# When the previous image's feed-forward runs inside the next image's convolution-attention, and where the weights are loaded

## Chip, core and metric

The kernel runs on one core of one Trainium2 chip. The metric is the time of one execution in microseconds of device time; the number to be predicted is the median of the runs. TensorE is called PE in the profile, VectorE DVE, ScalarE ACT, GpSimd POOL and SyncE SP. Matrix products read from SBUF and write to PSUM; every engine works through its own queue, and engines wait for one another through semaphores.

## The reference

Two layers on an input of 4 images with 128 channels and 64 x 64 = 4096 positions, all in float32. Cut to what matters:

```
# layer 0, per image: group norm (32 groups of 4 channels), 1x1 convolutions, attention over positions
g = groupnorm(x)                           # one mean and variance per 4 channels
e1, e2 = prelu(w1 @ g + b1), prelu(w2 @ g + b2)     # 64 x 4096
asm = prelu(wa @ g + ba)                            # 128 x 4096
x = x + softmax(e1.T @ e2, axis=2) @ asm.T

# layer 1, on tokens t = (position, channel)
z = layernorm(t) in 16 heads of 8; q = qz_ring(z + rx)      # cosines and running products
ctx = softmax(q @ q.T / sqrt(8)) @ q      # keys and values are q too
x1 = ln(layernorm(t) + ctx @ w_comb.T + b_comb) * g1 + be1
f  = relu((cos(x1[:8]) * cos(ry)) @ f1.T + fb1) @ f2.T + fb2
t2 = t + ln(x1 + f) * g2 + be2
# last: batch-normed linear map of layernorm(t2), then a sigmoid recurrence over tokens
out = t2 + scan(sigmoid(Wx_t + y @ V.T))
```

The attention runs over all 4096 tokens of an image, in 16 heads of 8 channels.

## The kernel before, in words

The four images go through three stages one after the other: first_stage (group norm, convolutions, the first attention, and from its results the tokens q), second_stage (the attention of 16 heads, the longest part) and third_stage (feed-forward). Only the last image has a third_stage of its own. The feed-forward of image n is otherwise run inside first_stage of image n + 1.

The order of the instructions on TensorE, ScalarE and VectorE within first_stage and second_stage is the order in which the program writes them (a manual schedule); TensorE executes in that order, so an instruction whose operand is late holds up what is behind it. In the rest of the program (the loads at the start, third_stage, the POOL and SP queues in first_stage) a planner chooses the order by its own estimates, with the program's order as priority.

Work is written as generators that yield between steps, so that pieces of several jobs can be laid between one another:

- layer0 (L324) is the main job of first_stage. It calls meanwhile after each of its groups: 4 calls in the e1 convolutions, 4 in e2, 4 in the asmT convolution (calls 1 to 12), then 16 calls for each of the 8 blocks of 512 positions (calls 13 to 140). In a block it writes two score products (L387, exponential on ScalarE L395, sum on VectorE L400 or L403), then one weighing (L410) of an earlier pair before each of the two calls; the first two calls come before there is anything to weigh.
- tokens (L468) makes the tokens of one block of 512 positions out of layer0's result, in 17 steps: transposes px, pt, layer norm, the cosines, products q (L542), transposes pq. One of them is begun every 16 calls, from call 30 on; each call takes one step of the oldest (two in the last block).
- feed_forward (L975) treats 512 tokens of the image before, in 27 steps (counted from 0): transposes pc and copy cT (0), product pw and sum v with x1 (1, L998), statistics (2), norm (4), z and cosines (6, 8), copy zs (9), transposes pz (11), products ph with relu to hT (13, 14), product pf (16), u and statistics (17), norm (19), t2 and statistics (21, L1071), norm of w (23, L1075), transposes pt2 with copy t2T and store to DRAM (24), transposes pl with the copy last or every (25), product pwx and its statistics (26). Its PSUM tiles come from a pool of two buffers.
- in_steps (L1169) keeps up to two feed-forwards active in first_stage and begins a new one every 14 steps; third_stage keeps up to eight and begins one every step. There the norms are done by ScalarE.
- mirrored (L769) ends the attention of a block: many small copies on POOL and a sum into own (L792). The last three blocks of an image leave three result functions (L797, L798: own divided by its denominators, into q), which first_stage calls at the calls named in L1206.

At the start, load (L135) and load_row issue all weights on POOL's queue: first w1, w2, b1, b2, wa, a1, a2, aa and ba; then the weights of later parts, rx to beta, 23 of them; then identity and constants; and last the group matrix grp, which two affine selects on POOL (L198) cut out of a constant. norm_stats (L303) needs it: image 0's two products pg and pv, on which its group norm hangs. PSUM pairs (ps_pair, two buffers) carry convolutions and scores alternately.

Of the kernel before, what the change touches and what calls it, by code (L numbers as in the profile page):

```python
# [10 lines left out]
F32 = mybir.dt.float32  # L11
F32R = mybir.dt.float32r
AF = mybir.ActivationFunctionType
ALU = mybir.AluOpType
# [12 lines left out]
def kernel(  # L27
# [32 lines left out]
    P = 128  # L60
# [71 lines left out]
    BIG, MID, HALF, ONE = (P, S), (P, 2, IC), (P, IC), (P, IC)  # L132


    def load(ap, name, shape=None):  # L135
        t = const.tile(list(shape or ap.shape), F32, tag=name, name=name)
        nc.gpsimd.dma_start(out=t, in_=ap)
        return t

    def load_row(ap, name):  # L140
        return load(ap.partition_broadcast(P), name, (P, ap.shape[-1]))
# [23 lines left out]
    for i, b in enumerate((b1_sb, b2_sb)):  # L165
        t = const.tile([P, 1], F32, tag=f"minus_b{i}", name=f"minus_b{i}")
        nc.vector.tensor_scalar(t, b, -1.0, None, ALU.mult)
        minus_b.append(t)
    rx_bc = load_row(rx, "rx_bc")
    wc_sb, bc_bc = load(w_combT, "wc_sb"), load_row(b_comb, "bc_bc")  # L170

# [2 lines left out]
    nc.gpsimd.memset(f1_sb, 0.0)  # L174
    nc.gpsimd.memset(ry_sb, 0.0)
    for f in range(NF):
        nc.gpsimd.dma_start(out=f1_sb[ds(32 * f, D), :], in_=f1T[:, ts(f, P)])
        nc.gpsimd.dma_start(out=ry_sb[ds(32 * f, D), :], in_=ry)
    fb1_sb, f2_sb, fb2_bc = load(fb1, "fb1_sb"), load(f2T, "f2_sb"), load_row(fb2, "fb2_bc")
    g1_bc, be1_bc = load_row(g1, "g1_bc"), load_row(be1, "be1_bc")  # L180
    g2_bc, be2_bc = load_row(g2, "g2_bc"), load_row(be2, "be2_bc")
# [10 lines left out]
    nc.vector.memset(half_pi, math.pi / 2)  # L192
    minus_half = const.tile([P, NT], F32, tag="minus_half", name="minus_half")
    nc.vector.memset(minus_half, -0.5)

    grp = const.tile([P, P // 4, 4], F32, tag="grp", name="grp")
    nc.vector.memset(grp, 0.25)
    for sign, base in ((1, 0), (-1, 3)):  # L198
        nc.gpsimd.affine_select(
            out=grp,  # L200
            in_=grp,
            compare_op=ALU.is_ge,
            fill=0.0,
            base=base,
            pattern=[[-4 * sign, P // 4], [0, 4]],
            channel_multiplier=sign,
        )
    grp = grp.rearrange("p a b -> p (a b)")

    V = D + 1  # L210
    t2_dram = dram.tile([N * P, S], F32, tag="t2", name="t2_dram")
# [763 lines left out]
    def feed_forward(im, i, t2_rows, last, final):  # L975


        n, cols = im["n"], ts(i, IC)

        def norm(dst, src, mv, rstd, name):  # L980
            if final:
                normalise_act(blocks(dst), blocks(src), mv, rstd, TG, f"{name}{n}_{i}")
            else:
                normalise(blocks(dst), blocks(src), mv, rstd, TG)

        x1 = get("x1", f"fx1_{n}_{i}")
        nc.sync.dma_start(out=x1, in_=im["x1"][:, cols])
        nc.gpsimd.tensor_tensor(blocks(x1), blocks(x1), row4(bc_bc), ALU.add)
        pt = transposed(blocks(im["q"][:, cols]), f"pc{n}_{i}")
        cT = get("fhalf", f"cT{n}_{i}")  # L990
        nc.scalar.copy(cT, pt)
        yield

        pa = one_psum(f"pw{n}_{i}")
        for k in range(TG):
            nc.tensor.matmul(pa[:, ts(k, P)], cT[:, ts(k, P)], wc_sb, start=True, stop=True)
        v = get("fhalf", f"v{n}_{i}")
        nc.vector.tensor_tensor(v, pa, x1, ALU.add)  # L998
        yield
        mv, rstd = token_stats(blocks(v), TG, 1e-5, f"v{n}_{i}")  # L1000
        yield
        yield
        norm(v, v, mv, rstd, "v")
        nc.gpsimd.tensor_tensor(blocks(v), blocks(v), row4(g1_bc), ALU.mult)
        nc.gpsimd.tensor_tensor(blocks(x1), blocks(v), row4(fb2_bc), ALU.add)
        yield
        yield

        z, zk, zr = (
            small.tile([P, TG, D], F32, tag=name, name=f"{name}{n}_{i}") for name in ("z", "zk", "zr")  # L1010
        )
        be1_z = be1_bc[:, 0:D].unsqueeze(1).broadcast_to([P, TG, D])
        nc.vector.tensor_tensor(z, blocks(v)[:, :, 0:D], be1_z, ALU.add)
        steps = cos_steps(zr, z, zk, zr)
        for _ in range(3):
            next(steps)
        yield
        yield
        next(steps, None)
        yield  # L1020
        zs = get("fhalf", f"zs{n}_{i}")
        nc.vector.tensor_copy(
            zs.rearrange("p (k r d) -> p k r d", k=TG, d=D),
            zr.unsqueeze(2).broadcast_to([P, TG, P // D, D]),
        )
        yield
        yield
        pz = transposed(blocks(zs), f"pz{n}_{i}")
        zT = get("fhalf", f"zT{n}_{i}")
        nc.scalar.copy(zT, pz)  # L1030
        yield
        yield
        hs = []
        for f0 in range(0, NF, 2):
            phs = [one_psum(f"ph{n}_{i}_{f}") for f in range(f0, f0 + 2)]
            hs.append(get("hT", f"hT{n}_{i}_{f0}"))
            for j in range(2):
                rows = ds(32 * (f0 + j), D)
                nc.tensor.matmul(phs[j], f1_sb[rows, :], zT[rows, :], start=True, stop=True)
            for j in range(2):  # L1040
                bias = fb1_sb[:, f0 + j : f0 + j + 1]
                nc.scalar.activation(hs[-1][:, j, :], phs[j], AF.Relu, bias=bias)
            yield
        yield
        x0 = get("fhalf", f"fx0_{n}_{i}")
        nc.sync.dma_start(out=x0, in_=im["x0"][:, cols])
        po = one_psum(f"pf{n}_{i}")
        for k in range(TG):
            for f in range(NF):
                nc.tensor.matmul(  # L1050
                    po[:, ts(k, P)],
                    hs[f // 2][:, f % 2, ts(k, P)],
                    f2_sb[:, f, :],
                    start=f == 0,
                    stop=f == NF - 1,
                )
        yield

        u = im["q"][:, cols]
        nc.vector.tensor_tensor(u, po, x1, ALU.add)  # L1060
        mv, rstd = token_stats(blocks(u), TG, 1e-5, f"u{n}_{i}")
        yield
        yield
        norm(u, u, mv, rstd, "u")
        nc.gpsimd.tensor_tensor(blocks(u), blocks(u), row4(g2_bc), ALU.mult)
        nc.gpsimd.tensor_tensor(blocks(u), blocks(u), row4(be2_bc), ALU.add)
        yield
        yield

        t2 = get("fhalf", f"t2_{n}_{i}")  # L1070
        nc.vector.tensor_tensor(t2, u, x0, ALU.add)  # L1071
        mv, rstd = token_stats(blocks(t2), TG, 1e-5, f"w{n}_{i}")
        yield
        yield
        norm(u, t2, mv, rstd, "w")  # L1075
        yield
        pt = transposed(blocks(t2), f"pt2_{n}_{i}")
        t2T = get("fhalf", f"t2T{n}_{i}")
        nc.scalar.copy(t2T, pt)
        nc.sync.dma_start(out=t2_rows[:, cols], in_=t2T)  # L1080
        yield
        pt = transposed(blocks(u), f"pl{n}_{i}")
        tokens_i = last(n, i, pt)
        yield
        if n != "r":
            token_products(n, i, tokens_i)
# [99 lines left out]
    def first_stage(im, before):  # L1186


        n = im["n"]


        ffn = dict(x1=(HALF, 2), fhalf=(HALF, 6), hT=(MID, 2))
        sums = dict(sums=(MID, 2), half=(HALF, 2), thalf=(HALF, 6))
        rest = dict(e=(BIG, 2), big=(BIG, 1), mid=(MID, 5))
        pools = {**ffn, "gap": ((P, GAP), 1), **rest, **sums}
        psum = dict(ps_acc=(ONE, 1), ps_pair=(MID, 2), ps_one=(ONE, 2), ps_tok=(ONE, 1))
        engines = {nc.tensor.engine, nc.scalar.engine, nc.vector.engine}
        with stage(f"conv{n}", **pools, **psum), tc.manual_schedule(engines=engines):
            nc.gpsimd.memset(get("gap", f"gap{n}")[:, 0:1], 0.0)
            own, calls = [], [0]  # L1200
            step_late = in_steps(feed_forwards(before) if before else [], 14, 2)

            def meanwhile(steps=1):

                calls[0] += 1
                if before and calls[0] in (13, 15, 17):  # L1206
                    before["left"].pop(0)()
                for _ in range(steps):
                    step_first(own)
                if calls[0] > 8:  # L1210
                    step_late()

            norm = im["norm"] or list(norm_stats(n, im["xs"]))[-1]
            layer0(
                n,
                im["xs"],
                im["q"],
                norm,
                n == "r",
                lambda ic, sums: own.append(tokens(im, ic, sums)),  # L1220
                meanwhile,
            )
            *own, tail = own
            for g in own:
                for _ in g:
                    pass
            while step_late():
                pass
            while not next(tail):
                pass  # L1230
        return tail
# [308 lines left out]
```

## Time and profile before

| what | us |
|---|---|
| median of 3 runs (7298.4 to 7300.03) | 7299.96 |
| the profiled execution itself | 7298.87 |
| its span in the profile | 7297.2 |
| image 0: scores, windows 59 to 435 us | 376 long, TensorE busy 370.5, mean clock 1.00 |
| image 1: scores with feed-forward, 1715 to 2222 us | 507 long, TensorE busy 462.9, mean clock 0.96 |
| image 2: the same, 3504 to 4010 us | 506 long, TensorE busy 469.2, mean clock 0.97 |
| image 3: the same, 5285 to 5785 us | 500 long, TensorE busy 456.0, mean clock 0.96 |
| pwx of the last feed-forward starts | 7185.48 |

Busy time is the time in which an engine executed; the clock is the share of TensorE's full rate that was granted. The windows' bounds are the first score product and about the first product of the attention that follows. In a timeline each row gives start, duration, engine, line, operation and count, and in brackets how long the engine had been idle before and what ended the wait. In a table of waits each row gives the waiting group, the group it waited for, the total in us, how many times, and the longest.

### The profile page before, as it was taken

What the parts mean: (1) busy time and instruction counts of PE and PEld (TensorE: products, weight loads), DVE (VectorE), ACT (ScalarE), POOL (GpSimd) and SP (SyncE); (2) the same over time, 40 slices, a digit from 0 to 9 for tenths busy, and PEclk for the clock granted to TensorE, in tenths of its full rate; (3) what the DMA queues carried; (4) which work ended last, traced back from release to release, by engine and by line L of the source; (5) the groups of instructions that cost most, each with busy time, mean ns of one, the idle gap of its engine ahead of it and who ended that gap; (6) DMA issues with size and microseconds to landing.
All of it is one profiled execution on the core that took longest, in us unless ns stands there. A gap on an engine that the chain in (4) does not pass through costs nothing. (4 is left out here: it accounts for less than half of the span.)

```text
span 7297.2 us, 224976 instructions
## 1 busy us (share of the span) xinstructions
PE 7005.9 (96%) x93198; PEld 3505.6 (48%) x93198; DVE 5997.3 (82%) x8097; ACT 5906.1 (81%) x11647; POOL 2795.8 (38%) x9860
## 2 busy tenths in 40 slices
PE   8999999999999999999989999999999999999977
PEld 3345555554444555554444455555444455555546
DVE  5678899886778899889677998889877788889974
ACT  3479999995448999999444999999844599999976
POOL 1024445333323444443423354444522343444542
PEclk9999999999999999999999999999999999999988
DMA  1010000000111000000011100000001110000012
GB/s 28 32 35 24 28 22 21 21 9 25 35 34 47 30 20 21 21 23 20 21 34 44 38 21 20 21 27 19 18 22 39 39 37 21 21 26 27 11 59 105
DMA packets 81598, 212.81 MB, mean 29 GB/s; under 512 B 8801, under 2 KB 8833, under 8 KB 79793
## 3 DMA queue, kind: packets, MB, share of 16 engines
q1 hardware_dynamic: 77312, 186.68, 7.5%
q8 instruction: 733, 12.01, 0.7%
q10 hardware_dynamic: 2016, 10.49, 0.4%
q14 instruction: 305, 2.49, 0.1%
q0 software_dynamic: 1232, 1.14, 0.1%
HBM read 141.65 MB, written 56.62 MB: 27 GB/s over the span
## 5 line engine op out<-in xcount | busy, mean ns | idle before, releaser
L882 ACT ACTIVATE e<-s 128x1024 f32<-128x1024 f32 (+1 forms) x3480 | 2946.7, 889 | 63.9 <-PE s L870 39.8
L689 DVE STREAM_TRANSPOSE t<-e 128x1024 f32<-128x1024 f32 x2240 | 2586.5, 1207 | 6.6 <-ACT e L882 4.3
L702 PEld LDWEIGHTS misc<-t,mirror 128*32 128x32 f32 x57344 | 1662.9, 110 | 1410.7 <-issue 1347.7
L702 PE MATMUL misc<-t,mirror 128*32 128x128 f32 x57344 | 1995.7, 273 | 28.5 <-DVE later L716 21.3
L882 ACT ACTIVATE xs<-s 128x1024 f32<-128x1024 f32 (+1 forms) x2152 | 1835.2, 893 | 32.8 <-PE s L870 19.6
L689 DVE STREAM_TRANSPOSE t<-xs 128x1024 f32<-128x1024 f32 x1344 | 1558.2, 1207 | 2.2 <-ACT xs L882 0.8
L723 PE MATMUL acc<-e,q_aug 128*32 128x512 f32 x11360 | 1518.4, 606 | 0.0
L870 PE MATMUL s<-queries,keys 32*128 32x512 f32 x9216 | 1218.3, 495 | 4.1 <-ACT e L882 2.7
L765 POOL COPY own<-o 32x36 f32<-32x36 f32 x2048 | 434.3, 212 | 1724.4 <-DVE o L757 1644.1
L395 ACT ACTIVATE p<-s 128x1024 f32<-128x1024 f32 x512 | 497.8, 1022 | 626.6 <-PE s L387 625.4
L410 PE MATMUL acc<-p,asmT 128*128 128x512 f32 x2048 | 981.3, 612 | 0.0
L723 PE MATMUL acc<-xs,q_aug 128*32 128x512 f32 x7072 | 942.2, 605 | 0.0
L403 DVE TENSOR_TENSOR total<-total,p 128x1024 f32<-128x1024 f32 x448 | 580.8, 1296 | 325.6 <-ACT p L395 301.8
L870 PEld LDWEIGHTS s<-queries,keys 32*128 32x128 f32 x9216 | 480.7, 182 | 491.3 <-issue 366.1
L790 POOL COPY other<-turned 32x64 f32<-32x64 f32 x1904 | 449.1, 236 | 631.3 <-DVE turned L780 552.8
L659 POOL COPY mirror<-q 32x128 f32<-32x128 f32 x2048 | 598.8, 292 | 239.1 <-PE misc L702 151.2
L882 ACT ACTIVATION_READ_ACCUMULATOR e<-s 128x1 f32 x2880 | 650.5, 226 | 0.0
L410 PEld LDWEIGHTS acc<-p,asmT 128*128 128x128 f32 x2048 | 364.6, 192 | 520.7 <-issue 516.1
L387 PE MATMUL s<-e,e 64*128 64x512 f32 x2048 | 526.6, 633 | 24.8 <-DVE asmT L301 21.2
L716 DVE TENSOR_TENSOR later<-later,misc 128x128 f32<-128x128 f32 (+1 forms) x576 | 162.4, 282 | 369.9 <-PE misc L702 365.9
L750 POOL COPY by_token<-by_key 32x4 f32<-32x4 f32 x2016 | 373.9, 185 | 85.0
L723 PEld LDWEIGHTS acc<-e,q_aug 128*32 128x32 f32 x11360 | 225.7, 108 | 347.8 <-issue 330.1
(258 smaller groups left out, 4764.0 us busy)
## 6 DMA issues: line engine op xcount, KB each, us to landing
keys<-parts_dram SPq DMA_DIRECT2D x256, 256.0 KB
queries<-parts_dram SPq DMA_DIRECT2D x1024, 32.0 KB
fx<-x_dram SPq DMA_DIRECT2D x64, 256.0 KB
x_dram<-x SPq DMA_DIRECT2D x56, 256.0 KB
xs<-in_x_dram SPq DMA_DIRECT2D x16, 512.0 KB
t_dram<-t2T SPq DMA_DIRECT2D x32, 256.0 KB
t2s<-t_dram SPq DMA_DIRECT2D x16, 512.0 KB
parts_dram<-high SPq DMA_DIRECT2D x28, 256.0 KB
```

The source lines that it names most:

```text
L387: nc.tensor.matmul(s[:, j, :], e2[rows, ts(2 * jp + j, P)], e1[rows, ts(ic, IC)], start=True, stop=True,)
L395: nc.scalar.activation(p, s, AF.Exp)
L403: nc.vector.tensor_tensor(state[ic], state[ic], p, ALU.add)
L410: nc.tensor.matmul(state["acc", ic], asmT[:, ts(2 * jp + j, P)], p[:, j, :], start=jp == 0 and j == 0, stop=jp == NP - 1 and j == 1,)
L659: nc.gpsimd.tensor_copy(wv[ts(a, 32), s, :, :, ts(a, D)], own[ts(s, 32)])
L689: nc.vector.transpose(group["e"][h][:, k, :], es[h])
L702: nc.tensor.matmul(state["acc"][ts(2 * x + h, 32), :], state["w"][:, QT * (s // 4) + TG * x + s % 4, h, :], state["e"][h][:, :, ds(IC * x ...
L723: nc.tensor.matmul(it["in"]["acc"][ts(2 * h + x, 32), :], it["qa"][:, ds((2 * it["tiles"][x] + h) * V, 32)], it["e"][h][:, ts(x, IC)], sta ...
L765: nc.gpsimd.tensor_copy(own[ts(s, 32), ts(x, 4), h, :], ov[ts(2 * h + x, 32), s, :, 0:V])
L790: copy(to[ts(k, 32), h], tv[ts(2 * x + h, 32), k])
L870: nc.tensor.matmul(ss[h][:, x, :], keys[unit[x] // QT].bitcast(F32R)[r, ts(unit[x] % QT, P)], queries[b].bitcast(F32R)[r, :], start=True, ...
L882: nc.scalar.activation(es[h][:, ts(x, IC)] if split else es[h], ss[h][:, x, :] if split else ss[h].rearrange("p x c -> p (x c)"), AF.Exp, ...
```

## The change

It has three parts. In the load code, grp is built right after the first weights, and the loads from rx to beta are issued by ScalarE instead of POOL (the two memsets that precede the loads of f1 and ry stay on POOL). In feed_forward, pt2 with its copy and store is put ahead of the norm of w, in the same step as that norm; the number of steps stays 27. In meanwhile, the feed-forward of the image before takes no step in calls 1 to 12 (before: 1 to 8), then one step in each call and two in every eighth; the second and third left result are called at calls 16 and 19 (before: 15 and 17).

```diff
+    loader = [nc.gpsimd]
     def load(ap, name, shape=None):
         t = const.tile(list(shape or ap.shape), F32, tag=name, name=name)
-        nc.gpsimd.dma_start(out=t, in_=ap)
+        loader[0].dma_start(out=t, in_=ap)
         return t
...
-    rx_bc = load_row(rx, "rx_bc")
...
-    nc.vector.memset(minus_half, -0.5)
     grp = const.tile([P, P // 4, 4], F32, tag="grp", name="grp")
...
     grp = grp.rearrange("p a b -> p (a b)")
+    loader[0] = nc.scalar
+    rx_bc = load_row(rx, "rx_bc")
+    wc_sb, bc_bc = load(w_combT, "wc_sb"), load_row(b_comb, "bc_bc")
...
+    nc.gpsimd.memset(f1_sb, 0.0)
+    nc.gpsimd.memset(ry_sb, 0.0)
+    for f in range(NF):
+        nc.scalar.dma_start(out=f1_sb[ds(32 * f, D), :], in_=f1T[:, ts(f, P)])
+        nc.scalar.dma_start(out=ry_sb[ds(32 * f, D), :], in_=ry)
...
+    nc.vector.memset(minus_half, -0.5)
@@ feed_forward
         yield
         yield
-        norm(u, t2, mv, rstd, "w")
-        yield
         pt = transposed(blocks(t2), f"pt2_{n}_{i}")
         t2T = get("fhalf", f"t2T{n}_{i}")
         nc.scalar.copy(t2T, pt)
         nc.sync.dma_start(out=t2_rows[:, cols], in_=t2T)
+        norm(u, t2, mv, rstd, "w")
+        yield
         yield
         pt = transposed(blocks(u), f"pl{n}_{i}")
@@ first_stage
                 calls[0] += 1
-                if before and calls[0] in (13, 15, 17):
+                if before and calls[0] in (13, 16, 19):
                     before["left"].pop(0)()
                 for _ in range(steps):
                     step_first(own)
-                if calls[0] > 8:
+                for _ in range(0 if calls[0] <= 12 else 2 if calls[0] % 8 == 0 else 1):
                     step_late()
```

## The prediction

> **What bounds the kernel now.** I read the page's busy table and slices first, then the timeline of the start, then the timelines and waits of TensorE in the stretches where feed-forward is mixed into the next image's first stage.
>
> ```profile
> PE 7005.9 (96%) x93198; PEld 3505.6 (48%) x93198; DVE 5997.3 (82%) x8097; ACT 5906.1 (81%) x11647; POOL 2795.8 (38%) x9860
> ...
> PE   8999999999999999999989999999999999999977
> ```
>
> TensorE is busy almost everywhere, so time is to be had only where it idles or runs slowly. The change touches four such places: the start, the three stretches of slices 10-12, 20-22 and 29-31, and the last feed-forward. In the long attention stretches the windows show TensorE busy for 181.9 us of 182 and nothing is changed.
>
> The start, from its timeline (columns: start us, duration us, engine, line, operation, count, idle before and its releaser):
>
> ```profile
> 9.15 0.54 POOL L137 DMA_DIRECT2D aa_sb<-in_aa_dram  x1 [0.27 <-DMA w_sb<-in_w2T_dram]
> ...
> 14.38 0.37 DVE L310 BATCH_NORM_AGGREGATE gmv<-gst 128x2 f32<-128x48 f32 x1
> ...
> 23.96 0.53 POOL L199 TENSOR_SCALAR_AFFINE_SELECT grp<-grp 128x128 f32<-128x128 f32 x1
> ...
> 24.54 0.58 PE L312 MATMUL pg<-gmv,grp 128*128 128x1 f32 x2 [24.54 <-POOL state L1433]
> ```
>
> The reader is to see that the statistics are there at 14.75 us, but the first matmul waits until 24.5 for the group matrix, which POOL makes only after issuing all loads at 0.50 to 0.58 us each. Everything after hangs on this matmul.
>
> The beginning of the scores of images 1 and 3, timelines of TensorE and VectorE:
>
> ```profile
> 1704.30 0.60 PE L273 MATMUL pc<-ident,q 128*128 128x128 f32 x4
> ...
> 1720.97 0.69 DVE L998 TENSOR_TENSOR v<-pw,fx 128x512 f32<-128x512 f32 x1 [10.45 <-POOL own L792]
> ...
> 1727.15 3.78 PE L387 MATMUL s<-e,e 64*128 64x512 f32 x8 [8.94 <-DVE asmT L301]
> ...
> 1735.70 1.99 PE L387 MATMUL s<-e,e 64*128 64x512 f32 x8
> ...
> 5297.61 3.78 PE L387 MATMUL s<-e,e 64*128 64x512 f32 x8 [9.18 <-DVE asmT L301]
> ```
>
> The second feed-forward step writes v (L998) while POOL still finishes the attention before it (its last mirrored sum, L792, ends at 1720.94). VectorE waits 10.45 us there with the last two asmT groups queued behind it; TensorE then waits 8.94 us for a PSUM buffer that asmT has to release. In image 2 the same place waits only 1.27 us.
>
> Inside the score loop, TensorE's waits of image 1 from 1727 us on:
>
> ```profile
> PE pl L273 <- DVE q L255: 11.8, 3, 4.4
> PE pq L273 <- DVE q L542: 9.2, 2, 6.2
> ...
> PE pc L273 <- ACT hT L1042: 5.4, 7, 0.8
> ...
> PE ph L1039 <- DVE wx_stats L1092: 2.1, 1, 2.1
> PE pt L273 <- DVE t L1071: 1.5, 2, 0.8
> ```
>
> These are moments when VectorE is two or more calls behind TensorE. The windows give TensorE 462.9 us busy of 507 in image 1's scores, at a mean clock of 0.96.
>
> **What the Trainium skill says.** (1) "TensorE: Matmul & The Clock Gate", Part 1: the array falls to half rate after an idle window of about 3.4 us and needs as long to recover. The trace agrees: after the wait of 8.94 us eight L387 matmuls took 3.78 us, otherwise 1.99. A wait above 3 us thus costs 2 to 3 us more. (2) The table that opens that page: ScalarE, VectorE and GpSimd have strictly first-in-first-out queues. That is the 10.45 us case. (3) "Trainium Kernel Development and Optimization", Key Constraints: DMAs from SP, ACT and POOL use the same 16 DMA engines, so another issuer saves issue time only. No run here shows a change of issuer for the same load; the trace shows 0.54 us for a POOL issue and a median of 0.47 us for ScalarE's loads of every.
>
> **The change part by part.**
>
> *Start.* 23 loads leave POOL's queue and the two selects of grp (0.55 + 0.53 us) come right after ba_row, whose issue ends at 10.69. So grp is there at about 11.8, before gmv at 14.75, and pg starts near 14.9: 24.5 - 14.9 = 9.6 us less. Now gmv is late next: its last two bn_stats stand in VectorE's queue behind the wait for aa_sb (landed 13.0). ScalarE issues 23 loads at about 0.47 us = 11 us; its first real work, L294, was at 31.7 and would be at 22. The loads of f1 wait for POOL's memset (now near 12 us), with the rest queued behind them: ScalarE is done near 12 + 20 x 0.47 = 21.4, just in time. The loads now overlap those of x: the windows show the DMA engines full (1.03) from 4 to 8 us. If aa_sb, or the fb_bc add and ry steps in VectorE's queue, land later, up to 6 us are lost. I take -8.5 (ends: -10 and -3).
>
> *First scores.* Calls 9 to 12 lose their steps: the transposes pc (0.60) and products pw (1.06) leave the asmT phase and come between the first score pairs. Worked out for image 1: asmT matmuls end at 1714.84 - 1.66 = 1713.2; two score pairs of 1.1 us with a wait of 1.1 for the exponential between them, 1716.5; pc 0.6; wait for cT on ScalarE (exponential 1.0 + copy 0.6) to 1718.3; pw 1.06; two pairs 2.0 and two weighings 3.7: the next L387 at 1725.1 against 1735.7. -10.6, half-clock included. VectorE still waits until 1720.94 for v, but reaches it only at 1719.4, with asmT done. The two left results (reciprocal and product, 0.25 + 0.29 us each) at calls 16 and 19 find POOL done. Image 3 the same, image 2 has only about -1 to gain. Sum -21 (ends -24 and -12).
>
> *Rate.* From call 13 on, one step a call and two in each eighth: after call c, c - 12 + floor(c/8) - 1 steps are done. Eight feed-forwards of 27 steps, 14 apart, need 7 x 14 + 27 = 125: before, the last was in call 133, now in call 123 of 140. The instructions are the same. What a doubled call does: two successive steps lie in one call, so a consumer follows its producer without a score pair between. The doubled steps are 9m - 15 and 9m - 14. By their place in the feed-forward those that hurt TensorE are 39/40 (pwx waits for the copy of pl, 1.09 us less 0.6 of pz: 0.5), 66/67 (pl one call closer to its norm; a call is about 4 us: 0 to 4, I take 2.5), 84/85 (pw waits for cT: 0.6) and 111/112 (the second ph waits for two relus of 0.6: 1.3). Sum 5 us per image.
>
> VectorE's lag: tokens use it in bursts, a new one every 16 calls from call 30 on. Of 27 feed-forward steps, 1 to 9 with 15 to 23 beside them carry nearly all of the 13.5 us of VectorE work. Before, pl falls 14, 12 and 10 calls after a token start in the three cases that wait, and 16, 8, 2 or fewer in those that don't. Now it falls at 5, 2, 14, 10, 7, 3, 16 and 12: again three in 10 to 14 and one at 16 (which waits at pq, 6.2). I take no difference. After call 123 there is no feed-forward: the late waits pt 1.54 and pq 3.02 go down to what image 0 has there (0.6 and 1.7): -2.3, with the clock -3. Loop: (5 - 3) x 3 = +6 (ends -10 and +60).
>
> *Order at the end of feed-forward.* The norm of w stays two steps ahead of pl; only the transposes pt2, their copy (0.6 us ScalarE) and store move one step earlier, ahead of that norm. They now follow t2 by two steps, not three. Where VectorE is three calls behind, TensorE waits at pt2 what it waited at pl (0.78 + 4.39 before); where it is between two and three behind, the wait is new. In the last stage ScalarE does that norm itself (1.64 us) and copies t2T (0.64) between it and pl; one copy leaves the chain of the last group: -0.6, against a possible wait for pt2. I take 0 (ends -2 and +3).
>
> Sum: -8.5 - 21 + 6 + 0 = -23.5. Profiled execution: 7298.87 (span 7297.2 and 1.7 around it) gives 7275; the median shown, 7299.96, lies 1.1 above, so about 7277.
>
> **Rivals.** A change under 0.2% (14.6 us here) can't be told from none by these measurements.
>
> *A: hidden anyway (no change), 7295.* The doubled steps cost 9 us per image (66/67 at 4, and pt2 two calls behind in 21/22), and the crowded loads give only 4 us at the start: -4 - 21 + 3 x (9 - 2) = -4. For: VectorE is 362 of 507 us busy in these loops, in bursts. Against: the waits at the first scores are large and their cause is moved away.
>
> *B: slower, 7330.* One mechanism: pt2 comes within two steps of t2 and doubled calls cut this to one, so TensorE, which takes its instructions in the written order, waits for VectorE at pt2 in most feed-forwards. Price: one call's slack is about 4 us, and a wait above 3 us brings 2.3 of half clock. Three new waits of 6.3 and the 9 of the doubled steps are 28 per image, 84 in all: 84 - 29.5 = +54; with one in three hidden, +30. It decides once VectorE is two to three calls behind in more than two of eight. For: two of eight were over three calls behind (pt 0.78 each). Against: the other six had no wait at pl, two steps after their norm.
>
> *C: the start is not earlier*, since ScalarE's loads hold up prelu: -21 + 6 = -15, 7285. It shifts the time and no sign.
>
> **How the numbers follow.** Forecast with C: 0.58; A: 0.22; B: 0.20. Forecast's own range: 7258 to 7290 (all gains at their ends; C at the other). To leave out two in ten at most, the range goes to 7318, which takes in A and the milder half of B. Faster by over 0.2%: the forecast without its upper edge, and a little of A: 0.57. Within: 0.25. Slower: 0.18.
>
> **What would show it.** Right: pg near 15 us; no wait above 2 us at asmT L301 in images 1 and 3; first L870 of each attention earlier by the sums; waits at pl, pt2 and pq together still 20 to 30 us per image. Wrong: pt2 <- t L1071 waits of several us, many pwx <- last and pw <- cT waits, the loops' windows longer than 507, 506 and 500 us less the 10 at their head, or prelu L294 waiting for ScalarE's issues.

## The result and the profile after

The changed kernel takes 7301.9 us (median of 12 runs, 7295.1 to 7310.9) against 7299.07 before (12 runs, 7297.8 to 7300.0): a ratio of 1.0004 with a 95% interval from 0.9996 to 1.0012. That is no change. The profiled execution spans 7299.6 us, 2.4 more than before.

A large change moved the time by nothing, so the first thing to do is to cut the span at marks that both kernels have, and to see which stretches grew and which shrank. The marks are the product pg of each image (the group norm), the third batch of eight score products (L387 before, L391 after), the first product of each attention (L870, L874), and the last pwx.

| stretch, us | before | after | difference |
|---|---|---|---|
| start to the first attention of image 0 | 435.3 | 429.1 | -6.2 |
| pg to the third batch of scores, images 1, 2, 3 | 59.9, 49.8, 60.2 | 50.5, 51.2, 50.5 | -17.5 |
| from there to the attention (the loop), images 1, 2, 3 | 486.7, 487.8, 486.3 | 497.0, 494.3, 496.1 | +26.5 |
| the four attentions up to the next pg or the last pwx | 5119.5 | 5118.3 | -1.1 |
| last pwx to the end | 111.7 | 112.4 | +0.7 |

The expected gains came, 24 us in two places. The score loops with feed-forward inside gave them back.

The page of the changed kernel, busy time and slices:

```profile
PE 7004.1 (96%) x93198; PEld 3502.2 (48%) x93198; DVE 6003.5 (82%) x8097; ACT 5911.8 (81%) x11648; POOL 2794.4 (38%) x9837
...
PE   8999999999899999999989999999999899999977
```

The busy times are those of before within 7 us on every engine. Nothing here tells that anything happened; the page's totals are the wrong view for a change of order.

The start in the timeline of the changed kernel:

```profile
0.83 8.05 SPq L1119 DMA_DIRECT2D xs<-in_x_dram  x4
...
15.39 0.15 DVE L166 TENSOR_SCALAR aa_sb<-aa_sb 128x1 f32<-128x1 f32 x1 [0.37 <-DMA aa_sb<-in_aa_dram]
...
17.29 0.56 PE L316 MATMUL pg<-gmv,grp 128*128 128x1 f32 x2 [17.29 <-DVE gmv L314]
...
25.58 1.28 ACT L246 ACT_TABLE_LOAD   x1
26.88 0.29 ACT L246 ACTIVATE cry<-cr,half_pi 128x1 f32<-128x1 f32 x1
```

pg now waits for the statistics, not for grp. It starts at 17.3, later than the 14.9 of the prediction, as aa_sb lands 2.4 us later and the last two statistics stand behind it on VectorE. SP also takes 8.05 us to issue the four loads of x, 1.82 before. Its waits tell why (waiting load, the load it waited for, total us, times, longest):

```profile
SPq L1119 <- DMA rx_bc<-in_rx_dram: 4.1, 1, 4.1
SPq L1119 <- DMA fb_sb<-in_fb_dram: 2.4, 1, 2.4
```

The third load of x waits until rx_bc has landed, and the fourth until fb_sb has. These are loads that ScalarE issued and that x does not need. In the trace each of the two loads of x waits for the semaphore that tells of the other's landing, and then uses that same semaphore for itself: the loads of both queues share a few semaphores in turn. The 6.5 us of these two waits cover the difference of 6.2. After pg another 1.1 us is lost: the sine cry now stands between two relus of prelu on ScalarE, with a table load of its own.

The first scores of image 1, TensorE and VectorE of the changed kernel:

```profile
1709.60 2.08 PE L391 MATMUL s<-e,e 64*128 64x512 f32 x4 [1.79 <-DVE asmT L305]
...
1713.40 1.16 PE L1000 MATMUL pw<-wc_sb,cT 128*128 128x128 f32 x8 [0.68 <-ACT cT L995]
1714.49 1.99 PE L391 MATMUL s<-e,e 64*128 64x512 f32 x8
...
1716.30 0.69 DVE L1002 TENSOR_TENSOR v<-pw,fx 128x512 f32<-128x512 f32 x1 [1.78 <-POOL own L796]
1716.40 3.70 PE L414 MATMUL acc<-p,asmT 128*128 128x512 f32 x8
```

v still waits for the same sum of POOL, but only 1.78 us, and behind it no asmT waits any more. The wait of 8.94 us at asmT is 1.79 now. The four products right after it still take 2.08 us, as long as eight usually take, but the next L391 runs at full rate (1.99 for eight). That is the step as predicted.

The waits of TensorE in image 1 of the changed kernel, from the asmT convolution to the attention (waiting group, releaser, total us, times, longest):

```profile
PE pt L277 <- DVE t L1075: 22.7, 5, 7.8
PE pc L277 <- ACT hT L1046: 5.4, 7, 0.8
PE pl L277 <- DVE q L259: 4.7, 2, 3.4
PE pq L277 <- DVE z L1017: 2.8, 1, 2.8
PE pq L277 <- DVE q L546: 1.9, 1, 1.9
...
PE pw L1000 <- ACT cT L995: 1.4, 2, 0.7
PE ph L1043 <- ACT hT L1046: 0.8, 1, 0.8
PE pwx L1095 <- ACT last L1154: 0.7, 1, 0.7
```

pt2 (the line of t, L1075) had 1.5 us of waits, now 22.7; pl and pq had 23.3 in their rows, now 9.4; the three together go from 24.8 to 32.1. This looks as if the new place of pt2 were the culprit, and that is the trap of this case: the experiments say no. The waits for ScalarE that the doubled calls were expected to bring (pw, ph, pwx) are there, and small.

What one such wait is made of, VectorE beside TensorE in image 1 of the changed kernel:

```profile
1861.77 1.23 DVE L407 TENSOR_TENSOR total<-total,p 128x1024 f32<-128x1024 f32 x1
1862.91 1.11 DVE L259 TENSOR_SCALAR x<-x,mv_t,r_t 128x128 f32<-128x128 f32 x4
...
1868.72 2.06 DVE L259 TENSOR_SCALAR v<-v,mv_v,r_v 128x128 f32<-128x128 f32 x4
...
1876.43 1.11 DVE L259 TENSOR_SCALAR q<-q,mv_u,r_u 128x128 f32<-128x128 f32 x4
1877.46 0.68 DVE L244 SCALAR_TENSOR_TENSOR r<-r 128x512 f32<-128x512 f32 x1
...
1881.72 0.94 DVE L1075 TENSOR_TENSOR t<-q,fx 128x512 f32<-128x512 f32 x1
...
1882.72 1.11 PE L277 MATMUL pt<-ident,t 128*128 128x128 f32 x4 [7.79 <-DVE t L1075]
1883.76 3.63 PE L391 MATMUL s<-e,e 64*128 64x512 f32 x8
```

From 1861.8 to 1882.7 VectorE has no idle time: a token's norm (x) and cosines (r), the older feed-forward's norm of u (q), the newer one's norm of v, and the sums of scores lie in one stretch. TensorE had only scores and weighings to do beside it and was through at 1874.9. After the wait the score products run near half rate, 3.63 instead of 1.99 us.

Not all of that stretch is work. Five of the instructions in it took longer than the same ones do where no GpSimd instruction runs beside them, about 5 us in all (an estimate from their durations in this loop): z (L1017) took 1.29 us, 0.18 in the one case of eight that has no GpSimd instruction beside it; the second sum of scores took 2.11, and 73 such sums with no GpSimd instruction beside them took 1.23 at most. No run varies this, so what it costs the loops is not shown. It does not explain the difference to the faster kernel below that has no doubled calls: there VectorE is busy for longer in this loop, 357.9 us against 354.8.

### The profile page after: what moved, and what is told of

The parts are those of the page before. It is cut to its first block, busy times and chain, and to the rows that moved or that the text cites. A ratio compares the mean times of both kernels' runs of the same rounds, so it can differ in the third digit from the quotient of the medians.

```text
span 7299.6 us, 224978 instructions
## 1 busy us (share of the span) xinstructions
PE 7004.1 (96%) x93198; PEld 3502.2 (48%) x93198; DVE 6003.5 (82%) x8097; ACT 5911.8 (81%) x11648; POOL 2794.4 (38%) x9837
## 5 line engine op out<-in xcount | busy, mean ns | idle before, releaser
L874 PE MATMUL s<-queries,keys 32*128 32x512 f32 x9216 | 1217.2, 495 | 3.9 <-ACT e L886 2.9
L874 PEld LDWEIGHTS s<-queries,keys 32*128 32x128 f32 x9216 | 480.9, 182 | 491.3 <-issue 373.4
L391 PE MATMUL s<-e,e 64*128 64x512 f32 x2048 | 533.4, 640 | 7.4 <-DVE asmT L305 7.1
```

Source lines behind the costliest of these rows:

```text
L391: nc.tensor.matmul(s[:, j, :], e2[rows, ts(2 * jp + j, P)], e1[rows, ts(ic, IC)], start=True, stop=True,)
L874: nc.tensor.matmul(ss[h][:, x, :], keys[unit[x] // QT].bitcast(F32R)[r, ts(unit[x] % QT, P)], queries[b].bitcast(F32R)[r, :], start=True, ...
```

## The experiments

Twelve kernels beside the two were measured, each against the kernel before on the same chip. As the changed kernel's time varies from run to run by up to 16 us, the loops are read from the profile, where three images repeat the same code. "First" and "loop" are sums over images 1 to 3 of the second and third stretch of the table above, "last stretch" is the last attention up to the last pwx. Each comes from one profiled execution. That execution lies within 4 us of the median in most kernels, but 8.4 us below it with a period of 12, 5.2 below with the order of pt2 undone, and 5.0 above with a period of 15.

| kernel | median us | ratio to before, 95% | first | loop | last stretch |
|---|---|---|---|---|---|
| before | 7299.1 | | 169.8 | 1460.9 | 1393.0 |
| changed | 7301.9 | 1.0004 (0.9996 to 1.0012) | 152.3 | 1487.4 | 1392.1 |
| order of pt2 undone | 7311.6 | 1.0016 (1.0009 to 1.0024) | 152.5 | 1490.1 | 1394.2 |
| no doubled calls | 7270.0 | 0.9961 (0.9947 to 0.9975) | 151.1 | 1456.3 | 1390.2 |
| both undone | 7274.6 | 0.9967 (0.9954 to 0.9979) | 153.4 | 1456.5 | 1393.2 |
| before, with grp early | 7295.8 | 0.9996 (0.9987 to 1.0004) | 169.3 | 1460.5 | 1392.9 |
| extra step only where it is empty | 7289.4 | 0.9985 (0.9978 to 0.9993) | 153.6 | 1477.6 | 1391.7 |
| doubled calls moved by four | 7316.8 | 1.0026 (1.0016 to 1.0037) | 150.7 | 1503.1 | 1391.7 |
| no doubled calls, start at call 9 | 7290.8 | 0.9988 (0.9981 to 0.9995) | 169.8 | 1460.8 | 1391.5 |
| no doubled calls, pt2 at pl | 7282.1 | 0.9976 (0.9967 to 0.9986) | 150.9 | 1466.2 | 1394.8 |
| no doubled calls, begun every 13 | 7300.9 | 1.0001 (0.9992 to 1.0009) | 151.9 | 1489.0 | 1391.7 |
| no doubled calls, begun every 12 | 7286.5 | 0.9983 (0.9976 to 0.9989) | 149.8 | 1468.6 | 1390.5 |
| doubled, then none: mean rate 1 | 7292.3 | 0.9991 (0.9982 to 1.0) | 151.8 | 1481.9 | 1391.5 |
| no doubled calls, begun every 15 | 7260.5 | 0.9945 (0.9929 to 0.9962) | 154.8 | 1438.8 | 1395.6 |

### Which part lost it: order or rate

Order of pt2 undone (the norm of w first again):

```diff
-        pt = transposed(blocks(t2), f"pt2_{n}_{i}")
...
         norm(u, t2, mv, rstd, "w")
         yield
+        pt = transposed(blocks(t2), f"pt2_{n}_{i}")
```

> The changed kernel with one part undone: the transposes pt2, their copy and store again one step after the norm of w (three steps after t2). Theory O (the loops lost 26 us because pt2 came within two steps of t2): the waits of TensorE at pt2 for t2 fall from 22.7 us per image to under 5, not all of it comes back at pl and pq, each loop gets 5 to 9 us shorter, time 7276 to 7288. Theory R (the doubled calls and the crowding lost it): the wait only moves from pt2 to pl, the loops stay within 2 us each, time 7297 to 7304.

Measured 7311.6, the loops 2.7 us longer in all, the last stretch 2.1 longer. Neither theory had the time. The profile shows about half of the 9.7 us between the medians, as this profiled execution was a quick one. The waits in image 1:

```profile
PE pl L277 <- DVE q L259: 11.9, 6, 6.8
PE pq L277 <- DVE q L546: 8.6, 2, 6.7
PE pt L277 <- DVE t L1075: 7.9, 3, 4.0
```

28.4 us in these three rows, 29.3 in the changed kernel: the wait had only moved. Theory O falls.

No doubled calls:

```diff
-                for _ in range(0 if calls[0] <= 12 else 2 if calls[0] % 8 == 0 else 1):
+                for _ in range(0 if calls[0] <= 12 else 1):
```

> The changed kernel with one step of feed-forward in each call from 13 on, no doubled calls; the new order of pt2 stays. Theory R: waits at pw, pwx and ph for ScalarE go (about 3 us per image) and those at pt2 fall below 10 us per image; each loop 5 to 9 us shorter, time 7276 to 7288. Theory O: pt2 still waits 15 us and more per image; loops shorter by 1 to 3 us each, time 7291 to 7300.

Measured 7270.0, loops 10.4 us shorter per image than in the changed kernel: theory R's direction, and more than its numbers. Its waits in image 1:

```profile
PE pt L277 <- DVE t L1075: 13.1, 3, 4.7
PE pc L277 <- ACT hT L1046: 5.4, 7, 0.8
PE pq L277 <- DVE q L546: 4.9, 1, 4.9
```

pt2 still waits three times, 13.1 us, which is between what the two theories said. With the new place kept, the whole loss is gone, so the new place of pt2 is not what costs, and the rate is. Added up over the three loops, TensorE was idle for 101.3 us before, 124.4 in the changed kernel and 88.9 here, and executed for 1359.6, 1363.0 and 1367.4 us: what the doubled calls cost the changed kernel is waiting, though no row of the table of waits names its cause.

Both undone, so that only loads and late start are left:

> The changed kernel with both undone: old order of pt2, one step in each call from 13 on. What is left of the change is the start and the later first step. Under either theory the loops go back to their lengths before the change: start -6, first scores -17.5, loops 0, time 7274 to 7282. A third theory P (what counts is where the feed-forwards fall against the token bursts, whatever order and rate): the four calls of shift alone change the waits, loops off by more than 4 us each in either direction, time outside 7270 to 7286.

Measured 7274.6, as said: loops as without doubled calls to 0.1 us, the last stretch 3.0 us longer. So the new order is worth nothing in the loops at a rate of one, 2 to 3 us in the last stage, and it helps where calls are doubled (7301.9 against 7311.6). The third theory P was not met here, but it comes back below.

### The start and the first scores, each alone

The kernel before with the group matrix moved and all loads left on POOL:

```diff
+    grp = const.tile([P, P // 4, 4], F32, tag="grp", name="grp")
...
     rx_bc = load_row(rx, "rx_bc")
```

> The kernel before with one edit: the group matrix is made right after the first weights, all loads stay on POOL. If the group matrix alone is the gain of the start: the first product with it at 15 to 18 us instead of 24.5 and the first attention product 6 to 9 us earlier than at 435.3, time 7290 to 7294. If POOL's queue of loads then holds the power function r_g or the constants that follow (identity, minus_half's user), the product is early but the normalised x waits on POOL until about 24 us: under 2 us gained, time 7297 to 7300.

The timeline of that kernel:

```profile
15.10 0.56 PE L312 MATMUL pg<-gmv,grp 128*128 128x1 f32 x2 [15.10 <-DVE gmv L310]
...
23.45 0.54 POOL L137 DMA_DIRECT2D beta_sb<-in_beta_dram  x1
...
24.25 0.58 POOL L228 TENSOR_TENSOR r_g<-v_g,minus_half 128x1 f32<-128x1 f32 x1
```

The first product is early (15.1, where the prediction had 14.9), but the power r_g stands on POOL behind the loads until 24.25; x is normalised from 24.87 instead of 27.31 and the attention begins 2.9 us earlier. The second case of the expectation was right in its mechanism, its gain was under-sized. SP's four loads of x take 1.82 us to issue here, as before the change. The issuer has to change as well for the 6.2 us, and the price of that is pg at 17.3.

One step per call, but from call 9 on:

```diff
-                for _ in range(0 if calls[0] <= 12 else 1):
+                for _ in range(0 if calls[0] <= 8 else 1):
```

> The changed kernel with one step per call and the first step of feed-forward in call 9 again, as before the change; loads and order of pt2 as changed. If the later first step is what saves 9 us in images 1 and 3 at their first scores: asmT waits of 9 us are back there, time 14 to 19 us above the same kernel with the start at call 13 (7270), so 7284 to 7289. If the wait was only moved: 7268 to 7274.

Measured 7290.8; the first scores are back at 169.8, 18.7 us longer. So the later first step is what saves them. The loops are 4.4 us longer as well (1460.8), which puts the time just above the range expected.

### What is wrong with the doubled calls

Two things come with them: a step loses a call between itself and its consumer, and feed-forwards follow one another more closely. First the other extra step, taken only where the second step holds no instruction:

```diff
+                if calls[0] > 12:
+                    step_late()
+                    taken[0] += 1
+                    if taken[0] % 14 == 10:
+                        step_late()
+                        taken[0] += 1
```

> The changed kernel with another extra step: it is taken once in 14 steps, where the second of the two steps holds no instruction (step 10 of the newer feed-forward, step 24 of the older), so a new feed-forward begins every 13 calls instead of 12.4 (every eighth call doubled) or 14 (none). Theory S (the doubled calls cost 32 us because a consumer loses a call of slack to its producer): the loss goes, 7267 to 7276. Theory C (crowding: VectorE's bursts of feed-forward and tokens meet more often or more densely when feed-forwards follow one another faster): between 7276 and 7296.

Measured 7289.4, loops 7.1 us longer per image than without. The time fits C, but it does not settle it: an empty step is slack too. Skipping it brings pl within one call of its norm, and pl waits 9.3 us there.

The doubled calls moved by four:

> The changed kernel with its doubled calls moved by four (20, 28, ... instead of 16, 24, ...): same rate, other steps fall into the doubled calls. If the loss is a matter of the rate alone: 7297 to 7307, waits for VectorE 30 us and more per image again. If it is a matter of which steps are doubled: off by more than 8 us in either direction.

Measured 7316.8, loops 5.2 us per image longer than with the calls at multiples of eight. Same rate, the same number of doubled calls: which steps they hold, or where they fall against the tokens, counts.

Doubled calls with the next call left out, so that a feed-forward begins every 14 calls as without them:

```diff
+                for _ in range({0: 2, 1: 0}.get(calls[0] % 8, 1) if calls[0] > 12 else 0):
```

> The changed kernel with its doubled calls kept (16, 24, ...) but no step in the call after each, so the mean rate is one step per call and feed-forwards begin every 14 calls. Theory S: the doubled calls alone cost most of what they cost in the changed kernel: 7285 to 7302. Theory C: 7267 to 7276.

Measured 7292.3: loops 25.6 us longer in all than without doubled calls, of the 31.1 in the changed kernel. Here feed-forwards follow one another as without doubled calls, so doubled calls, each with an empty call behind it, cost by themselves. Their wait table for image 1:

```profile
PE pt L277 <- DVE t L1075: 13.0, 3, 4.7
PE pq L277 <- DVE q L546: 4.8, 1, 4.8
PE pc L277 <- ACT hT L1046: 4.1, 6, 0.8
```

The first two are the rows of the kernel without doubled calls, nearly to the tenth, and the third is lower, though the loop is 5.8 us longer in this image. Over the three loops TensorE is idle for 9.4 us more and executes for 16.2 us longer. Its mean granted clock in them falls from 0.965 to 0.955, worth about 15.7 us (an estimate: the lost share of the clock times the length, 66.7 against 51.0). So here most of the loss is slower products, which no row of waits holds.

A closer period without lost slack: one step per call, a feed-forward every 13 or 12 calls, up to three active.

```diff
-            step_late = in_steps(feed_forwards(before) if before else [], 14, 2)
+            step_late = in_steps(feed_forwards(before) if before else [], 13, 3)
```

> The changed kernel with one step per call (all the slack between producers and consumers) but a new feed-forward every 13 calls instead of 14, up to three active. Theory C (crowding): loops 4 to 9 us longer per image than with 14, as in the run that skipped the empty step: 7282 to 7296. Theory S (lost slack): loops within 2 us of those with 14, 7266 to 7276.

> The same with a new feed-forward every 12 calls, slightly closer than in the changed kernel (12.4), with full slack. Theory C: loops 8 to 14 us longer per image, 7294 to 7312. Theory S: 7266 to 7280.

Measured 7300.9 with 13: loops 10.9 us per image longer than with 14, no call doubled. With 12 they are 4.1 us longer, less than the 8 to 14 of theory C, while the time is above what theory S allowed; the profiled run of that kernel spans 7276.3, the median of its 20 runs is 7286.5, so 4.1 is rather too low. A closer period alone can cost as much as the whole change lost, and the cost does not grow steadily: every 13 is worse than every 12. A period also shifts the feed-forwards against the tokens and against one another, so these two runs do not show that density is what costs.

In the kernel with 12 the named waits are 24.9 us in image 1, fewer than the 37.4 without doubled calls, and its loop is longer all the same. Slower products are not the reason, as the mean clock in this loop is 0.96 in both. The products ph are: they take 33.1 us of TensorE's time in this loop, 23.0 without doubled calls and 18.6 in the changed kernel. The two kernels' timelines, the changed one first:

```profile
1898.68 1.13 PE L1043 MATMUL ph<-zT,f_sb 8*128 8x512 f32 x4
```

```profile
1899.10 0.60 PE L277 MATMUL pl<-ident,q 128*128 128x128 f32 x4
1899.63 1.12 PE L1043 MATMUL ph<-zT,f_sb 8*128 8x512 f32 x2
1900.92 1.12 PE L1043 MATMUL ph<-zT,f_sb 8*128 8x512 f32 x2 [0.16 <-ACT last L1154]
```

In the changed kernel the two products ph of a step run at the same time; their four records take 1.13 us together. With a period of 12 the step of pl (25) falls into the same call as the first step of ph (13) of the next feed-forward. They share the pool of two PSUM buffers, the second product waits for ScalarE's copy last out of pl, and the two run one after the other. The waiting is in the weight loads of ph (for ScalarE's hT and last, 14.7 us in this loop) and mostly not in the rows of TensorE's waits.

In the same kernel, slow products follow short waits:

```profile
1890.53 0.66 PE L277 MATMUL pz<-ident,zs 128*128 128x128 f32 x4 [1.60 <-DVE zs L1026]
1891.12 3.63 PE L391 MATMUL s<-e,e 64*128 64x512 f32 x8
```

After a wait of 1.60 us (and 2.21 at pt2 just before it) the next score products take 3.63 us instead of 1.99.

### Two more places for the pieces

pt2 in the step of pl, four steps after t2:

> The changed kernel with one step per call and pt2 moved the other way, into the step of pl, four steps after t2 (two and three in the kernels compared so far). If slack for pt2 were what counts in the loops: shorter than with two steps, 7262 to 7268. If VectorE's lag is paid once in any case, at pt2 or at pl or at pq: loops within 2 us each, and the last stage 3 us longer, as with the old order: 7272 to 7278.

Measured 7282.1: loops 3.3 us per image longer, the last stretch 4.6 longer. Both theories missed the loops. With more slack for pt2 they got longer: the waits are now pq 11.0 and pl 9.8 in image 1, where the kernel without doubled calls has pq 4.9 and pt2 13.1. Of the three places tried at a rate of one, the nearest has the shortest time; why is not shown.

A feed-forward every 15 calls:

> The changed kernel with one step per call and a new feed-forward every 15 calls: its pc then no longer follows the second ph of the one before in the same call, so the seven waits of 0.8 us for hT per image should go (-5), but 132 steps don't fit into 128 calls and the last four, with pt2, pl and pwx, run after the scores with nothing beside them (+4 to +8 per image). Even or slightly worse than with 14: 7268 to 7282. If the phase against the tokens (16 calls) helps more than that: below 7266.

Measured 7260.5, 0.9945 of the kernel before: the lowest median of all, from four runs. Its waits for hT at pc, 5.4 us in image 1 of the kernel without doubled calls, are gone:

```profile
PE px L277 <- DVE low L562: 8.2, 3, 4.4
PE s L874 <- DMA queries<-parts_dram: 7.1, 2, 6.6
PE pl L277 <- DVE q L259: 5.5, 2, 3.7
```

The last feed-forward does overrun the scores, and the attention's loads are late by 6.6 us once, so the attention of image 1 is 5.8 us longer than without doubled calls (1249.5 against 1243.7) and gives a part back; the loops win 5.8 us per image all the same. The profiled execution, the slowest of the four, spans 3.5 us less than that of the kernel without doubled calls; the medians differ by 9.6. Whether it is the missing pc wait or the better phase against the tokens (16 calls) was not separated.

## Why the prediction was right in its range and wrong in its sum

The measured 7301.9 us lies in the range of 7258 to 7318 because that range had been widened to take in the rivals. The forecast's own range, 7258 to 7290, does not hold it. So the range came true, but the forecast of 7277 and its account of the loops did not. Of the signs named for being right one was met, the wait at asmT (1.79 us); pg was at 17.3 instead of near 15, the attention of image 3 began 2.6 us later instead of earlier, and pt2, pl and pq together waited 32.1 us instead of 20 to 30. Of the signs of being wrong, waits of several us at pt2 and longer loops came; the many waits at pwx and pw did not.

- *Start.* Predicted -8.5, measured -6.2. The step is right; the late landing of aa_sb (pg 17.3, not 14.9), which the prediction had named as a risk, and the late cry are the missing 2.3 us, inside the ends given.
- *First scores.* Predicted -21, measured -17.5: -9.3 and -9.7 in images 1 and 3 where -10.6 was worked out, +1.4 in image 2 where -1 was taken. The cause, asmT queued behind v on VectorE, is shown by moving the start back alone.
- *Loop.* This is the step that failed: "Loop: (5 - 3) x 3 = +6" was mis-sized, it measures +26.5. Two terms of it are wrong; the third came about, as the late waits of image 1 fell from 4.6 us to 2.5. The doubled calls, "Sum 5 us per image", cost 8.5 per image with the mean rate kept at one. The sum priced four waits in isolation. In that run 3.1 of the 8.5 are idle time of TensorE and the other 5.4 are longer execution, which the sum left out. And for the closer spacing "I take no difference" was read from the call numbers of pl alone; periods of 13 and 12 cost 10.9 and 4.1 per image without any doubled call, so counting alignments this way predicted nothing here.
- *Order of pt2.* Predicted 0 with ends of -2 and +3; in the profiles it is -3.0 in the last stage at a rate of one, -2.1 with doubled calls, and in the loops 0 and -2.7. By the medians of whole runs it is -4.5 and -9.7, beyond the end of -2. The slow rival B named this order as its mechanism. Its wait did appear, 22.7 us in image 1, but with the old order as much is waited at pl, pq and pt2 together. Rival B falls by its mechanism.
- *The rivals.* The time is that of rival A (7295 forecast, 7302 measured): gains at the head, given back in the loops. Its price for the doubled calls, 9 per image, is close to the 8.5 measured at a mean rate of one; that they are lost in the steps it names (pl one call closer, pt2 two calls behind) is not shown, so the agreement may be luck.

What stays open: how the loops' loss divides between lost slack and spacing in the changed kernel (of its 31.1 us, doubled calls alone cost 25.6, and a closer period alone 32.7 or 12.3, so they do not add), and why the period of 13 is worse than 12.

## What to carry to other kernels

Where one engine runs hand-ordered pieces of several jobs, judge an interleave by the length of the loop between two marks and not by one row of the table of waits: a wait moves to another row, it can lie in the weight loads, and what follows it can run slower. Moving a start behind the work that blocks it was predictable to a few us; a denser rate was not, so try the plain rate first and change the period by itself. A change of two gains and one loss that sum to nothing hides a better kernel: here leaving out the doubled calls gives 0.9961, and a period of 15 gives 0.9945.

## What the runs showed that was not expected

SP's issue of the four loads of x grew from 1.82 to 8.05 us when ScalarE issued loads beside it. This is 6.5 us of waiting for two of ScalarE's loads to land, through shared semaphores, so here a load that was given to another queue held up the first queue too. And waits well under 3 us are sometimes followed by slow products: after 1.79 us at asmT in image 1 of the changed kernel, four score products took 2.08 us instead of 1.13, while after 1.80 us at the same place in image 0 eight took the usual 1.99. With a period of 12, 2.21 and 1.60 us close together were followed by 3.63 instead of 1.99. The prediction counted that only for waits above 3 us, after the idle window of about 3.4 us that the Trainium skill names ("TensorE: Matmul & The Clock Gate", Part 1). Here the measurement decides: shorter waits can cost more than their length too.
